# Two-operand masks in layer 1 of a graph attention network: the node index read from a column of PSUM

## The chip, the cores and the metric

The kernel runs on one core of one Trainium2 chip. The metric is the device time of one execution, in microseconds (us); smaller is better. The times given are medians of several executions.

A core has five engines that take their instructions each from a queue of its own, in order: PE (TensorE, the matrix unit, whose weight loads are listed apart as PEld), DVE (VectorE), ACT (ScalarE), POOL (GpSimd) and SP, which here only issues transfers. SBUF and PSUM are the two on-chip memories, of 128 partitions each; matrix products land in PSUM. Sixteen DMA engines move data between DRAM and SBUF. An ordinary DMA is issued by SP or ACT. An *indirect* DMA, which fetches rows of a table by a list of indices, is issued by POOL, and the profile shows it as a POOL instruction (`DMA_INDIRECT`) with a duration.

## What is computed

6250 nodes with 768 features each, 100000 edges (sorted by destination) and a loop on each node. Features are normalised and clipped at zero, then two graph attention layers of 256 channels run over the edges (4 heads, then 1), then two dense layers, and the input is added:

```python
h = jnp.maximum(_layernorm(x, axis=-1), 0.0)
h = relu(gat_conv(h, src, dst, W1, a_src1, a_dst1, b1, heads=4))
h = relu(gat_conv(h, src, dst, W2, a_src2, a_dst2, b2, heads=1))
out = x + relu(h @ Wm1 + bm1) @ Wm2 + bm2

def gat_conv(x, src, dst, W, a_src, a_dst, bias, heads):
    h = (x @ W).reshape(n, heads, -1)
    e = leaky_relu((h * a_src).sum(-1)[src] + (h * a_dst).sum(-1)[dst], 0.2)
    e = exp(e - segment_max(e, dst)[dst])
    alpha = e / (segment_sum(e, dst)[dst] + 1e-16)
    return segment_sum(h[src] * alpha[:, :, None], dst) + bias
```

## The kernel before

**Three stages follow one another.** The first reads the features, normalises them, multiplies by `W1` and stores a table in DRAM: a row of 268 numbers for each node (`store1`, line 499). The second is the attention of layer 1 over the edges; it ends each block of 128 nodes with a product by `W2` and writes a second table (lines 1036 to 1064). The third is the attention of layer 2, with the dense layers and the output.

**Edges come in tiles of 128, four tiles to a group, two groups to a unit.** There are 782 tiles with edges, 196 groups and 98 units; a unit has the edges around one half block of nodes, and four groups make a block step `t`. In both layers `layer_edges` (line 642) runs a loop over the groups. `gather(g)` (line 666) issues one indirect DMA per tile, line 680, which fetches the 128 rows of the table that the tile's edges start from. It is called 8 groups ahead (`AHEAD`), and the tile `G` that takes the rows has 10 buffers. In 23 groups of layer 1 two of the four tiles were fetched during the first stage, from the part of the table that existed then, and laid aside in DRAM (`soon_rows`, `soon_away`); they are loaded back by SP (line 319), and rows that did not exist yet are put in by a one-hot product (`soon_hits` line 333, `soon_missing` line 344, `soon_whole` line 351). So layer 1 has 736 gathers on line 680, layer 2 has 762, and between them stand 20 gathers of line 371 that serve layer 2 in the same manner.

**What a group needs in layer 1.** `make_hot` (line 704) compares the numbers 0 to 127 along a row with the edge's destination: a one-hot matrix, edges by nodes, which adds edge rows up by node on PE. The other direction, a number of the destination node for each edge, takes the transposed one-hot matrix, nodes by edges: that is the *mask*. `make_mask(u)` (line 687) makes it for a unit of 8 tiles: `drow` holds the destinations, taken modulo 128, of 2048 edges in bf16, the same in all partitions (`fetch_rows`, line 640, from SP), and each partition compares them with its own number, `pidx`, a column of SBUF with the values 0 to 127. The result is 128 x 1024 in bf16 and goes to PE in `meet` (line 727), to ACT (line 739) and back to DVE (line 746). Masks are made five to six groups ahead of the group that uses them, one for two groups, in the middle of an iteration (lines 944 to 948).

On DVE a group then has two small operations on the attention factors (lines 761 and 762), the weighting of the gathered rows (line 764, `hw`, which is the last reader of `G`), and on PE the product with the one-hot matrix into `o_ps` (line 784). Line 802 carries sums on from unit to unit.

**Order.** From line 425 on, the instructions of an engine run in the order in which the program issues them; each engine waits on semaphores for what it reads and for buffers to come free.

**Constants in PSUM.** A bank of PSUM, `both_ps` (lines 130 to 139), is divided by `part_ps` into `iota_ps` (0 to 127 along the row), `nid_ps` (node numbers), `mine_ps` and `rden_ps` (work space), and what is left is `own_ps`, which holds, four numbers a block, the weights of the nodes' own loops. `keep_own` (line 1015) fills `own_ps` first and the rest of another bank after it.

Of the kernel before, what the change touches and what calls it, by code (L numbers as in the profile page):

```python
# [14 lines left out]
ALU = mybir.AluOpType  # L15
AX = mybir.AxisListType

P = 128
# [9 lines left out]
NT = -(-N // P)  # L28
# [43 lines left out]
def kernel(  # L72
# [21 lines left out]
    nc = tc.nc  # L94
# [22 lines left out]
    pidx = const.tile([P, 1], F32, name="pidx")  # L117
# [9 lines left out]
    late_nid = min(SOON_FROM, NEXT_FROM)  # L127
    wide = 4 * (HID // 4 + 1)
# [3 lines left out]
    def part_ps(n):  # L132
        at_ps[0] += n
        return both_ps[:, at_ps[0] - n:at_ps[0]]

    iota_ps, nid_ps, mine_ps, rden_ps = (part_ps(n) for n in (P, NT - late_nid, wide, 8))
    own_ps = part_ps(4 * P - at_ps[0])
    nc.vector.tensor_copy(iota_ps, iota)
    nc.vector.tensor_copy(nid_ps, nid[:, late_nid:])
    eps_c = const.tile([P, 1], F32, name="eps_c")  # L140
    nc.vector.memset(eps_c, EPS)
    idle = const.tile([P, 4 * P], BF16, name="idle")
# [483 lines left out]
    drow, mask = {}, {}  # L626
# [15 lines left out]
    def layer_edges(layer, H, node, pre, matched, pre_pool):  # L642
# [4 lines left out]
        with tc.tile_pool(name=f"eg{layer}", bufs=6) as eg, \  # L647
# [36 lines left out]
            def both(u):  # L684
                return tiles(2 * u)[0], TPG + tiles(2 * u + 1)[-1] + 1

            def make_mask(u):

                if layer == 2 or not 0 <= u < NU:
                    return  # L690
                a, b = (t * P for t in both(u))
                mask[u] = maskp.tile([P, 8 * P], BF16, name="mask")
                at = u % 2 * 8 * P
                nc.vector.tensor_scalar(mask[u][:, a:b], drow[u // 2][:, at + a:at + b], pidx, None,
                                        ALU.is_equal)

            def make_hot(g):

# [150 lines left out]
            if layer == 1:  # L849
                fetch_rows(0)  # L850
                soon_away(0)
                for r in range(1, 3):
                    fetch_rows(r)
                soon_sources(pre_pool, 0)
                fetch_rows(3)
                for u in range(4):
                    make_mask(u)
            else:
                next_away()
# [55 lines left out]
            for g in range(NG):  # L915
# [20 lines left out]
                if j == 0:  # L936
                    if layer == 1:
                        fetch_rows(t + 4)
                    node.prefetch(t)
                    if layer == 1:  # L940
                        meet(t + 2 if t > 0 else 1)
                elif j == (2 if t < NT - 1 else 1):
                    node.ahead(t)
                elif j % 2 and (layer == 2 or t > 0):
                    make_mask((g + (11 if layer == 1 else 7)) // 2)
                if layer == 1 and t == 0:
                    for u in ((), (4, 5), (6,), (7,))[j]:
                        make_mask(u)
                    if j == 1:
                        parts_out(1)  # L950
                    if j == 2:
                        meet(2)
# [576 lines left out]
```

## Time and profile before

| | |
|---|---|
| median of 3 executions | 2093.42 us (2092.66 to 2094.27) |
| the profiled execution, its own time | 2094.35 us |
| span of the profile, first to last instruction | 2092.6 us |
| mean granted TensorE clock | 0.918 |
| busy share | PE 77%, PEld 59%, DVE 71%, ACT 20%, POOL 73% |
| first stage | 0 to about 166 us |
| gathers of layer 1 | 166 to 1091 us |
| masks | 98, from 174 to 1036 us |
| gathers of layer 2 | 1116 to 2069 us |

A page of the profile sums busy time by engine, and lists groups of equal instructions with their count, busy time and mean duration in ns; behind the bar stand the idle time of the engine ahead of them and what ended it. Register, branch and semaphore instructions and the issuing of ordinary DMAs do not count as busy. In a timeline each row is one instruction or a run of equal ones: its start and duration in us, the engine, the line, the operation, what it writes `<-` what it reads, and in brackets the idle time before it. "issue" there is time in which the engine waited for nothing that the profile shows.

### The profile page before, as it was taken

How to read it: one execution, taken by the hardware profiler on the slowest of the kernel's cores; microseconds unless marked ns; L12 is line 12 of the kernel's file. 1: busy time of each engine (PE TensorE's matmuls, PEld its weight loads, DVE VectorE, ACT ScalarE, POOL GpSimd, SP SyncE). 2: the span in 40 equal slices, each digit the busy share in tenths (PEclk: the TensorE clock that was granted, in tenths of full speed). 3: DMA queues.
4: the chain of work that ended last, by engine and by line, in shares of the span. 5: the costliest groups of instructions: out<-in, count | busy, mean ns of one | idle time of the engine just before them, and what ended most of it. 6: DMA issues, size and time to landing. Idle time of an engine off the chain costs nothing.

```text
span 2092.6 us, 23253 instructions
## 1 busy us (share of the span) xinstructions
PE 1612.2 (77%) x7207; PEld 1228.4 (59%) x7208; DVE 1491.2 (71%) x2879; ACT 422.9 (20%) x1322; POOL 1521.5 (73%) x1666
## 2 busy tenths in 40 slices
PE   8984879878877887887763787777787787777676
PEld 6873657757666766766652655555555455454444
DVE  7855777777777777777763877777677677676774
ACT  5761111111111111111120111111111111111211
POOL 7067777777777777777777777777777777777774
PEclk9996989989989989999886899999999989999999
DMA  9998555555555555555447355455455555555453
GB/s 346 352 347 289 143 159 155 149 159 156 161 154 150 156 156 164 154 143 163 132 122 219 105 159 160 141 156 159 145 151 160 147 150 159 146 149 152 145 160 104
DMA packets 145643, 354.58 MB, mean 169 GB/s; under 512 B 33943, under 2 KB 57582, under 8 KB 145510
## 3 DMA queue, kind: packets, MB, share of 16 engines
q0 software_dynamic: 75040, 210.90, 36.9%
q1 hardware_dynamic: 69100, 140.62, 19.7%
q10 hardware_dynamic: 1370, 1.48, 0.3%
q8 instruction: 59, 0.97, 0.2%
q14 instruction: 74, 0.61, 0.1%
HBM read 311.29 MB, written 41.59 MB: 169 GB/s over the span
## 4 chain that ended last, share of the span: by engine, by line
POOL 22%; DMA 21%; PE 19%; DVE 19%; issue 17%; ACT 1%; DVEq 0%; SPq 0%; POOLq 0%; ACTq 0%
POOL G L680 22%; DMA G<-table,src_i 18%; PE o_ps L784 8%; PE h_ps L472 4%; DVE u_ps L775 3%; PE missing L344 3%; DVE hw L764 3%; DVE u_ps L777 3%; DVE hot L778 2%; PE y_ps L1184 2%; DVE hot L704 1%; DVE soon_hit L333 1%; DMA xTt<-in_xT 1%; DMA xt<-in_x 1%; PE missing L402 1%
## 5 line engine op out<-in xcount | busy, mean ns | idle before, releaser
L680 POOL DMA_INDIRECT G<-table,src_i x1498 | 1421.6, 949 | 456.3 <-issue 373.2
L784 PE MATMUL o_ps<-G,hot 128*128 128x258 f32 x1564 | 424.1, 418 | 257.1 <-DVE hot L778 256.7
L784 PE MATMUL o_ps<-hw,hot 128*128 128x260 f32 x1564 | 442.3, 436 | 165.7 <-DVE hw L764 138.1
L784 PEld LDWEIGHTS o_ps<-G,hot 128*128 128x128 f32 x1564 | 304.8, 203 | 369.6 <-DVE hot L778 322.4
L784 PEld LDWEIGHTS o_ps<-hw,hot 128*128 128x128 f32 x1564 | 327.1, 215 | 244.8 <-DVE hw L764 152.4
L811 ACT ACTIVATE sum<-acc 32x260 f32<-32x260 f32 (+1 forms) x384 | 160.0, 417 | 1362.0 <-DVE acc L802 1297.6
L775 DVE TENSOR_TENSOR u_ps<-rho_ps,G 128x512 f32<-128x512 f32 (+1 forms) x197 | 136.3, 692 | 234.3 <-DMA G<-table,src_i 163.4
L704 DVE TENSOR_TENSOR hot<-iota_ps,dcol 128x512 f32<-128x512 f32 x392 | 265.7, 679 | 0.0
L764 DVE TENSOR_TENSOR hw<-G,factors 128x1040 f32<-128x1040 f32 (+1 forms) x198 | 242.2, 1223 | 14.3 <-DVE factors L762 0.9
L344 PE MATMUL missing<-kept,soon_hit 128*128 128x268 f32 x1028 | 245.6, 395 | 0.0
L344 PEld LDWEIGHTS missing<-kept,soon_hit 128*128 128x128 f32 x1028 | 196.5, 193 | 36.1
L1184 PE MATMUL y_ps<-wm,mT 128*128 128x384 f32 x392 | 160.1, 533 | 0.8 <-ACT mT L1179 0.8
L761 DVE TENSOR_TENSOR factors<-G,factors 128x16 f32<-128x16 f32 (+1 forms) x198 | 34.5, 174 | 151.4 <-DMA G<-table,src_i 106.9
L472 PE MATMUL h_ps<-w,r 128*128 128x264 f32 (+1 forms) x588 | 137.1, 387 | 6.4 <-ACT r L462 6.3
L777 DVE TENSOR_TENSOR u_ps<-u_ps,G 128x512 f32<-128x512 f32 (+1 forms) x197 | 136.7, 694 | 6.8
L778 DVE TENSOR_TENSOR hot<-hot,u_ps 128x512 f32<-128x512 f32 (+1 forms) x197 | 134.1, 681 | 6.8
L472 PEld LDWEIGHTS h_ps<-w,r 128*128 128x128 f32 x588 | 108.0, 190 | 28.4 <-ACT r L462 9.6
L1184 PEld LDWEIGHTS y_ps<-wm,mT 128*128 128x128 f32 x392 | 70.5, 200 | 50.0 <-issue 25.0
L309 POOL DMA_INDIRECT G<-table,soon_i x46 | 43.7, 949 | 75.7 <-DMA xt<-in_x 53.6
L802 DVE SCALAR_TENSOR_TENSOR acc<-acc,keep,o_ps 128x260 f32<-128x260 f32 (+1 forms) x192 | 91.5, 477 | 5.0 <-PE o_ps L784 5.0
L333 DVE TENSOR_TENSOR soon_hit<-soon_of,iota_ps 128x1408 f32<-128x1408 int32 (+18 forms) x46 | 75.1, 1633 | 0.0
L1188 DVE TENSOR_TENSOR y<-y_ps,xt 128x384 f32<-128x384 f32 (+1 forms) x98 | 54.0, 551 | 26.7 <-PE y_ps L1184 26.3
(428 smaller groups left out, 1317.2 us busy)
## 6 DMA issues: line engine op xcount, KB each, us to landing
xt<-in_x SPq DMA_DIRECT2D x96, 384.0 KB, 5.4
drow<-dmod_d SPq DMA_DIRECT2D x49, 512.0 KB, 5.7
G<-table,src_i POOLq DMA_INDIRECT x1498, 2.8
xTt<-in_xT SPq DMA_DIRECT2D x49, 384.0 KB, 7.4
out<-y SPq DMA_DIRECT2D x48, 384.0 KB, 3.0
table<-kept SPq DMA_DIRECT2D x49, 134.0 KB, 4.3
table<-kept SPq DMA_DIRECT2D x49, 129.5 KB, 3.0
soon_d<-G SPq DMA_DIRECT2D x23, 268.0 KB, 7.7
```

What stands on the lines that cost most here:

```text
L333: nc.vector.tensor_tensor(soon_hit[k][:, :m], soon_of[i][:, t * P:(t + 1) * P].unsqueeze(1).to_broadcast([P, m, P]), nid_ps[:, SOON[i] - l ...
L344: nc.tensor.matmul(soon_p[k], hit[:, T - there], kept[T], start=(T == there), stop=(T == NT - 1))
L472: nc.tensor.matmul(h_ps[:, :n], r[:, k], w1[:, k, :n], start=(k == 0), stop=(k == KI - 1))
L680: nc.gpsimd.indirect_dma_start(out=G[g][:n, t], out_offset=None, in_=table[layer], in_offset=bass.IndirectOffsetOnAxis(ap=src_i[:n, k:k + ...
L704: nc.vector.tensor_tensor(hot[g][:, T[0]:T[0] + n], iota_ps.unsqueeze(1).to_broadcast([P, n, P]), dcol[:, k:k + n].unsqueeze(2).to_broadca ...
L764: nc.vector.tensor_mul(hw[:, of], Gg[:, :, :RW[1]].rearrange("p t (h c) -> p t h c", h=H), w.unsqueeze(3).to_broadcast([P, n, H, C + 1]))
L775: nc.vector.tensor_mul(u_ps[:, of], row.unsqueeze(1).to_broadcast([P, n, P]), e2.to_broadcast([P, n, P]))
L777: nc.vector.tensor_max(u_ps[:, of], u_ps[:, of], e1.to_broadcast([P, n, P]))
L778: nc.vector.tensor_mul(hot[g][:, of], hot[g][:, of], u_ps[:, of])
L784: nc.tensor.matmul(o_ps[u], hot[g][:, k], r, start=(g % 2 == 0 and k == 0), stop=(g % 2 == 1 and k == tiles(g)[-1]))
L811: nc.scalar.activation(done[t][r], acc[r], AF.Copy)
L1184: nc.tensor.matmul(y_ps, mT[:, j], wm2[:, j, s * half:(s + 1) * half], start=False, stop=(j == KH - 1))
```

## The change

A column is set aside in the PSUM bank and filled once, at the start, with the partition's number (`pidx_ps`). `make_mask` no longer compares `drow` with a number per partition (`tensor_scalar`, the number read from `pidx` in SBUF) but with this column, spread over the row with a step of zero, as a second operand (`tensor_tensor`). What comes out is the same. `own_ps` becomes one column narrower, 95 in place of 96, so that it holds the numbers of 23 blocks in place of 24; the others go to the second bank.

```diff
-    iota_ps, nid_ps, mine_ps, rden_ps = (part_ps(n) for n in (P, NT - late_nid, wide, 8))
+    iota_ps, nid_ps, mine_ps, rden_ps, pidx_ps = (part_ps(n) for n in (P, NT - late_nid, wide, 8, 1))
     own_ps = part_ps(4 * P - at_ps[0])
     nc.vector.tensor_copy(iota_ps, iota)
     nc.vector.tensor_copy(nid_ps, nid[:, late_nid:])
+    nc.vector.tensor_copy(pidx_ps, pidx)
...
-                nc.vector.tensor_scalar(mask[u][:, a:b], drow[u // 2][:, at + a:at + b], pidx, None,
-                                        ALU.is_equal)
+                nc.vector.tensor_tensor(mask[u][:, a:b], drow[u // 2][:, at + a:at + b],
+                                        pidx_ps.to_broadcast([P, b - a]), ALU.is_equal)
```

## The prediction

> **What bounds the kernel now.** I read four views: the summary of stages (busy time of each engine in chosen windows), the list of groups, the waits, and last single rows of the timeline. The summary first; its columns are the window, its length, the busy time and count of each engine, the granted clock, the DMA share and GB/s.
>
> ```profile
> 0.00:166.10 166.10, 146.23 (x657) 117.31 (x658) 118.52 (x286) 109.43 (x345) 80.96 (x148) 0.98 0.99 346
> 166.10:1090.70 924.60, 739.25 (x3656) 600.67 (x3656) 680.96 (x1386) 144.17 (x523) 700.44 (x736) 0.90 0.56 158
> 1090.70:1115.70 25.00, 8.48 (x24) 5.52 (x24) 7.10 (x26) 3.76 (x17) 18.92 (x20) 0.62 0.75 206
> 1115.70:2069.00 953.30, 704.41 (x2814) 496.97 (x2815) 676.70 (x1164) 162.03 (x427) 721.16 (x762) 0.93 0.52 152
> 2069.00:2092.60 23.60, 13.85 (x58) 7.89 (x56) 7.91 (x20) 3.56 (x11) 0.00 (x0) 0.95 0.11 36
> ...
> L680 POOL DMA_INDIRECT G<-table,src_i x1498 | 1421.6, 949 | 456.3 <-issue 373.2
> ```
>
> The engines stand in the order PE, PEld, DVE, ACT, POOL. In the first stage the DMA engines are busy at 0.99. After it nothing is: in layer 1 PE has 739 of 925 us, DVE 681, POOL 700. POOL seems to have a quarter of its time free, but the group row of the gathers says that it hasn't: 1498 gathers of 949 ns leave 456 us idle, which is 0.30 us a gather. The table of waits shows that this gap is no wait on another engine:
>
> ```profile
> POOL G L680 <- issue: 373.2, 1225, 0.3
> POOL G L680 <- PE o_ps L784: 20.4, 67, 0.3
> ```
>
> The last number is the longest single idle time: 0.3 us, whichever releaser the view names. So each gather takes its duration and 0.3 us between two, back to back from 166 to 2069 us. POOL's row of gathers is the path of 1903 of the 2093 us, and a microsecond saved in it is one of the total, as long as it stays ahead.
>
> **Where masks touch that row.** Layer 1 and a stretch of layer 2 in which no mask runs, for line 680 alone:
>
> ```profile
> 166.10:1090.70 924.60, 700.44 (x736) 0.90 0.56 158
> 1190.00:2069.00 879.00, 664.67 (x703) 0.95 0.52 152
> ```
>
> A gather in layer 1 takes 700.44 / 736 = 0.9517 us, in layer 2 664.67 / 703 = 0.9455 us. The time from one start to the next is 924.60 / 736 = 1.2563 against 879.00 / 703 = 1.2504 us. By durations layer 1 loses 736 x 0.0062 = 4.6 us, by starts 736 x 0.0059 = 4.3 us. Where it loses them, the rows say:
>
> ```profile
> 166.02 0.36 DVE L620 TENSOR_TENSOR v<-e,rho 128x196 f32<-128x196 f32 x1 [2.02 <-ACT e L618]
> 166.11 1.09 POOL L680 DMA_INDIRECT G<-table,src_i  x1 [0.30 <-issue]
> ...
> 183.76 1.01 POOL L680 DMA_INDIRECT G<-table,src_i  x1 [0.30 <-issue]
> 184.17 0.88 DVE L694 TENSOR_SCALAR mask<-drow,pidx 128x1024 bf16<-128x1024 bf16 x2 [9.23 <-DMA drow<-dmod_d]
> ...
> 378.34 0.47 DVE L694 TENSOR_SCALAR mask<-drow,pidx 128x1024 bf16<-128x1024 bf16 x1
> 378.43 1.21 POOL L680 DMA_INDIRECT G<-table,src_i  x1 [0.30 <-issue]
> 378.74 2.55 DVE L333 TENSOR_TENSOR soon_hit<-soon_of,iota_ps 128x2304 f32<-128x2304 int32 x1
> 379.94 0.95 POOL L680 DMA_INDIRECT G<-table,src_i  x1 [0.30 <-issue]
> ...
> 1035.77 0.98 POOL L680 DMA_INDIRECT G<-table,src_i  x1 [0.30 <-DVE o L1048]
> ```
>
> A gather that starts while a mask is in flight takes 1.21 us in place of 0.95 (at 378.43); one that a mask meets later in its course, 1.01 (at 183.76). I went through all starts of layer 1: up to the last mask 40 gathers are 0.03 us or more late, 39 of them with a mask beside them (the first at 183.76 us, the last at 1035.77), and the other is the very first, 0.14 us late beside line 620, which reads two tensors of SBUF. The 39 come to 4.4 us. The other masks cost POOL nothing; where they ran longer than the 0.47 us of the one at 378.34, they themselves waited:
>
> ```profile
> L694 DVE TENSOR_SCALAR mask<-drow,pidx x98: 407/477/723, 174.0 to 1036.2; 128x1024 bf16<-128x1024 bf16 x97, 128x768 bf16<-128x768 bf16 x1
> ```
>
> These are the shortest, the median and the longest of the 98, in ns (the shortest is the last, of 768 columns). So mask and gather hold something against each other that the next form doesn't: line 333 at 378.74 us compares SBUF with a spread PSUM column in 2.55 us, the very form of the new mask, and the gather that starts under it at 379.94 us takes 0.95 us.
>
> **The change part by part.** *The mask's hold on the gathers goes.* Adding up single gathers gives 4.4 us, the two window sums 4.6 and 4.3, less the 0.14 of line 620: 4.5 and 4.2. I take 4.4 and keep 4.2 to 4.5. The lower bound supposes that the new form holds no gather, as the row of line 333 shows.
>
> *The mask gets longer.*
>
> ```profile
> L694 DVE TENSOR_SCALAR mask<-drow,pidx 128x1024 bf16<-128x1024 bf16 x97 | 49.5, 513 | 15.6 <-DMA drow<-dmod_d 15.6
> ...
> L333 DVE TENSOR_TENSOR soon_hit<-soon_of,iota_ps 128x1024 f32<-128x1024 int32 x2 | 2.4, 1206 | 0.0
> ```
>
> Line 333 at the same 1024 columns takes 1206 ns, with 4-byte elements on both sides. For bf16 against a 4-byte column the trace has no row; the bounds are 513 ns (as now) and 1206, or a little above, and I take 1206, the row nearest in form. That adds 98 x 0.69 = 68 us to DVE in layer 1: 681 becomes 749 of 920 us.
>
> The Trainium skill speaks against the change here: "VectorE: DVE Perf Modes", section "The perf-mode tier table", puts `tensor_scalar` on bf16 in SBUF at four elements a cycle and any `tensor_tensor` with a PSUM operand at one. The rows agree in kind (513 against 1206 ns), and with the whole difference on the path the sum would be the second rival's.
>
> *What hides the 68 us.* Queued behind a mask on DVE are the group's factors and `hw`, and PE's products wait for those; POOL waits for `hw` only through the buffers of `G`. In the view of line 761 in layer 1 (idle time in us, times, by releaser) stands how far DVE keeps up:
>
> ```profile
>   DMA G<-table,src_i: 106.9, 71
> ```
>
> 71 times DVE had nothing to do until a gather landed. Its other large wait, from the view of line 351:
>
> ```profile
>   PE missing L344: 40.3, 20
> ```
>
> How late `hw` comes after its group's last gather, at the worst of the 190 groups that I followed after the start (group 19) and at an ordinary one (group 22):
>
> ```profile
> 260.35 0.95 POOL L680 DMA_INDIRECT G<-table,src_i  x1 [0.31 <-issue]
> ...
> 269.96 1.24 DVE L764 TENSOR_TENSOR hw<-G,factors 128x1040 f32<-128x1040 f32 x1
> ...
> 275.41 0.95 POOL L680 DMA_INDIRECT G<-table,src_i  x1 [0.30 <-DMA G<-table,src_i]
> ...
> 278.81 1.24 DVE L764 TENSOR_TENSOR hw<-G,factors 128x1040 f32<-128x1040 f32 x1
> ```
>
> 8.7 and 2.5 us after the gather's end, and it falls back to 2.4 or so within every eight groups. A gather issued eight groups ahead needs a buffer that was read two groups ago, which leaves it more than 30 us of its 40. A unit, two groups or 10 us, gets 0.69 us longer, out of idle time of (925 - 681 - 40) / 98 = 2.1 us. So `hw` gets later by one or two us at times and POOL does not see it; the cover would be gone at a mask of 0.5 + 2.1 = 2.6 us. At the start of layer 1 seven masks stand close together, 5 us more for DVE, but there some 40 gathers, 50 us, run before one needs a buffer that group 0 has read.
>
> *The new column.* One copy, of one column:
>
> ```profile
> 7.81 3.53 PE L509 MATMUL warm_ps<-idle 128*128 128x512 bf16 x8
> 7.83 0.18 DVE L139 COPY iota_ps<-nid 128x20 f32<-128x20 f32 x1
> ...
> 8.01 0.95 DVE L460 TENSOR_TENSOR cent<-xTt,mean_ps 128x768 f32<-128x768 f32 x1
> ...
> 9.00 0.84 ACT L462 ACTIVATE r<-cent 128x768 f32<-128x768 f32 x1 [0.90 <-DVE cent L460]
> ```
>
> 0.18 us at most, ahead of line 460. What needs that result on PE stands behind warm-up products until 11.34 us, and line 460 and ACT's 0.84 us after it would be done by 10.0: nothing, or 0.18 without that cover. The loops' numbers of block 23 move to the other bank; line 1030 reads them there, and takes 428 ns from either:
>
> ```profile
> L1030 DVE TENSOR_TENSOR iota_ps<-kept,factors 128x260 f32<-128x260 f32 x25 | 10.7, 428 | 0.1
> L1030 DVE TENSOR_TENSOR iota_ps<-kept,iota_ps 128x260 f32<-128x260 f32 x24 | 10.3, 428 | 0.0
> ```
>
> *What is late next.* When layer 1's gathers end sooner, 20 gathers of line 371 follow and then those of layer 2, which need the whole second table.
>
> ```profile
> 1097.52 5.29 SPq L1063 DMA_DIRECT2D table<-kept  x2
> ...
> 1115.76 0.95 POOL L680 DMA_INDIRECT G<-table,src_i  x1 [0.30 <-issue]
> ```
>
> The last store is issued by 1102.8 us, the first gather of layer 2 starts at 1115.76 without a wait. The last mask is at 1036 us, so both ends move together. The 23.6 us after the last gather do not change.
>
> The sum: 2092.6 - 4.4 = 2088.2 us of span, 2089.95 for the profiled execution, whose own time is 2094.35. That execution is 0.9 us above the median, so of the median: 2093.42 - 4.4 = **2089.0 us**, 0.21% less. The three executions before lie 1.6 us apart, and about 0.2%, 4.2 us, is what a measurement of this kernel can tell from no change: the gain sits on that line.
>
> **The rivals.** *The change doesn't do what it says*: any DVE instruction, or the longer one, meets as many gathers, and the masks hold as much as before: 2093.4. Against it stands the gather at 379.94 us; for it, that the new form has run here only on int32 and float32. 7%.
>
> *DVE becomes the bound*: with 68 us on the path, 2093.4 - 4.4 + 68 = 2157. For it: DVE at 74% of layer 1 rises to 81%, with PE waits on top. Against: 0.3 us is POOL's longest wait. 2%.
>
> *The new form takes the shared thing for its whole, longer run*, slower than before. The place is the start of a gather, the price is in these rows:
>
> ```profile
> 1180.40 0.96 DVE L1096 TENSOR_TENSOR drow<-dst_f,wbase 128x784 f32<-128x784 f32 x1
> 1180.75 1.44 POOL L680 DMA_INDIRECT G<-table,src_i  x1 [0.31 <-issue]
> ```
>
> A `TENSOR_TENSOR` of 0.96 us held a gather for 0.49. 98 such holds are 48 us, 2093.4 - 4.4 + 48 = 2137. It decides by whether the second operand comes through the way that gathers use: lines 620 and 1096 read two tensors of SBUF and hold, line 333 reads one of SBUF and one of PSUM and does not, and the new mask is of the second kind. 3%.
>
> The Trainium skill, "SBUF — State Buffer", section "Who interferes with whom", has the same split: an instruction with two SBUF inputs meets GpSimd's reads, one with at most one does not, outside the modes that use two ports. By that rule the hold goes, and the trace agrees (0.95 us at 379.94).
>
> **How the numbers follow.** The forecast has 88%. Around 2089.0 I put half a microsecond of the measured spread and a few tenths for the bounds, so 62% of it lies below 2089.2, the line of 0.2%: faster 0.55, same 0.88 x 0.38 + 0.07 = 0.40, slower 0.05. The range takes 1.7 us below the forecast, and above it nearly three, towards the case without gain: 2087.3 to 2091.8.
>
> **What would show it right or wrong.** Right: no gather of layer 1 above 1.0 us but the first; 920.2 us from the first gather to line 371; the mask's row at 1.2 us; DVE at 749 us in layer 1; POOL's longest wait still 0.3. Wrong: gathers of 1.2 us or more beside a mask (the form holds), or idle time of POOL on `hw` (buffers), or a gap at the first gather of layer 2.

## The result, and the profile after

| | before | changed | ratio, 95% interval |
|---|---|---|---|
| first comparison, 17 executions each | 2092.66 us | 2089.00 us | 0.9982, 0.9976 to 0.9989 |
| second comparison, another chip | 2094.93 us | 2090.57 us | 0.9983, 0.9973 to 0.9993 |

The medians lie 3.7 us apart in the first and 4.4 us in the second comparison; by the ratios the gain is 0.18 and 0.17%. The forecast of 2089.0 us was met. The gain is real, both intervals exclude 1, and it lies at the line of 0.2% as foreseen, though just below it, where the prediction had given the side above the better chance (0.55 against 0.40).

The windows of the changed kernel, cut at its own first gather (165.31 us) and at the first gather of line 372 (1085.64), first for all engines, then a stretch of layer 2 for its line 681 alone, which is line 680 of before:

```profile
165.30:1085.60 920.30, 730.13 (x3656) 595.36 (x3656) 746.83 (x1386) 144.23 (x523) 696.14 (x736) 0.91 0.56 159
...
1185.00:2063.00 878.00, 664.14 (x703) 0.94 0.52 152
```

POOL's 736 gathers of layer 1 take 696.14 us in place of 700.44, which is 0.9459 us each, against 664.14 / 703 = 0.9447 in layer 2: the difference between the layers is gone but for 0.0012 us. From the first gather to the end of the row it is 920.3 us in place of 924.6; in the trace of the second comparison (164.30 to 1085.23) it is 920.9. DVE has 747 us in place of 681 and pays for the change without being on the path. The mask's row in the list of groups:

```profile
L695 DVE TENSOR_TENSOR mask<-drow,iota_ps 128x1024 bf16<-128x1024 bf16 x98 | 118.1, 1207 | 15.1 <-DMA drow<-dmod_d 15.1
```

The views name a bank of PSUM by its tile, so `pidx_ps` stands there as `iota_ps`. 1207 ns is the mean, and the row of line 333 had said 1206. And a mask in flight while gathers start, in the timeline:

```profile
367.08 1.21 DVE L695 TENSOR_TENSOR mask<-drow,iota_ps 128x1024 bf16<-128x1024 bf16 x1
368.07 0.95 POOL L681 DMA_INDIRECT G<-table,src_i  x1 [0.30 <-issue]
```

This gather starts 0.22 us before the mask ends and takes 0.95 us. Of the 98 longer masks 95 are in flight at such a start, and every one of those gathers takes 0.94 to 0.96 us.

The span of the profile fell from 2092.6 to 2087.4, by 5.2 us, which is more than the medians show. Cut at the starts of gathers, the 5.2 are: 0.8 in the first stage, whose end lay anywhere from 164.3 to 167.7 us in the runs below on the chips on which before takes about 2094 us; 4.3 in the gathers of layer 1; 0.5 in those of layer 2, from an effect that was not forecast (below); and 0.5 given back after the last gather.

### The profile page after: what moved, and what is told of

It is laid out like the page before. It is cut to its first block, busy times and chain, and to the rows that moved or that the text cites. A ratio compares the mean times of both kernels' runs of the same rounds, so it can differ in the third digit from the quotient of the medians.

```text
span 2087.4 us, 23253 instructions
## 1 busy us (share of the span) xinstructions
PE 1604.8 (77%) x7206; PEld 1226.5 (59%) x7208; DVE 1557.0 (75%) x2880; ACT 423.1 (20%) x1322; POOL 1517.2 (73%) x1666
## 4 chain that ended last, share of the span: by engine, by line
POOL 21%; PE 21%; DVE 21%; DMA 19%; issue 16%; ACT 1%; DVEq 0%; SPq 0%; POOLq 0%; ACTq 0%
POOL G L681 21%; DMA G<-table,src_i 16%; PE o_ps L785 8%; PE h_ps L473 4%; PE missing L345 4%; DVE hw L765 3%; DVE u_ps L776 3%; DVE u_ps L778 3%; DVE hot L779 2%; DVE soon_hit L334 2%; PE y_ps L1185 2%; DVE hot L705 2%; DVE mask L695 1%; DMA xt<-in_x 1%; PE missing L403 1%
## 5 line engine op out<-in xcount | busy, mean ns | idle before, releaser
L785 PE MATMUL o_ps<-hw,hot 128*128 128x260 f32 x1564 | 435.0, 430 | 169.3 <-DVE hw L765 145.9
L695 DVE TENSOR_TENSOR mask<-drow,iota_ps 128x1024 bf16<-128x1024 bf16 x98 | 118.1, 1207 | 15.1 <-DMA drow<-dmod_d 15.1
L762 DVE TENSOR_TENSOR factors<-G,factors 128x16 f32<-128x16 f32 (+1 forms) x198 | 34.5, 174 | 78.6 <-DMA G<-table,src_i 57.4
```

Source lines behind the costliest of these rows:

```text
L695: nc.vector.tensor_tensor(mask[u][:, a:b], drow[u // 2][:, at + a:at + b], pidx_ps.to_broadcast([P, b - a]), ALU.is_equal)
L785: nc.tensor.matmul(o_ps[u], hot[g][:, k], r, start=(g % 2 == 0 and k == 0), stop=(g % 2 == 1 and k == tiles(g)[-1]))
```

## Experiments

The theory: a gather waits at certain moments while DVE runs an operation of certain forms; the old mask was one of them and the new is not; the longer mask is hidden by DVE's idle time. Rivals: that it matters where the number `pidx` is read rather than the form; that two operands as such are harmless; that the longer mask already eats part of the gain. Four kernels ran first on a chip on which the kernel is slower, and were repeated on others.

### Where the number is read

```diff
-                nc.vector.tensor_tensor(mask[u][:, a:b], drow[u // 2][:, at + a:at + b],
-                                        pidx_ps.to_broadcast([P, b - a]), ALU.is_equal)
+                nc.vector.tensor_scalar(mask[u][:, a:b], drow[u // 2][:, at + a:at + b], pidx_ps, None,
+                                        ALU.is_equal)
```

> The number per partition is read from the PSUM column, but as the scalar of a one-tensor operation, as before the change. Theory (what holds the gathers is the fast run of a one-tensor operation from SBUF to SBUF, wherever its scalar lies): the masks take 0.47 us again, about 40 gathers of layer 1 are late, layer 1's gathers take 924 to 925 us to line 372, the time is that of before, 2092.7. Rival (the SBUF column pidx is what is held): masks of 0.47 us and no late gather, 920.3 us, 2088 to 2089.

> The scalar form with its number read from the PSUM column, once more. Theory (the fast one-tensor run from SBUF to SBUF is what holds gathers, wherever the scalar lies): masks of 0.47 us, 35 to 45 late gathers in layer 1 that come to 3.5 to 5 us, layer 1's gathers 924 to 925.5 us, the time of before within 1.5 us. Rival (reading pidx from SBUF holds them): no late gather beside a mask, 920.3 us, 4 us less than before.

On the slower chip 2604.8 us against 2607.3 of before, ratio 1.0005 (0.9979 to 1.0032), which decides nothing. On the other 2093.52 against 2094.16, ratio 0.9997 (0.9988 to 1.0006): no gain. The windows of line 681 there:

```profile
167.70:1091.40 923.70, 699.46 (x736) 0.91 0.57 158
```

923.7 us, near the 924.6 of before and 3.4 above the changed kernel, a little under the expected 924; 28 gathers beside masks are 0.03 us or more late, by 2.9 us in all, under the expected 35 to 45 and 3.5 to 5 us. One of them:

```profile
352.33 0.48 DVE L695 TENSOR_SCALAR mask<-drow,iota_ps 128x1024 bf16<-128x1024 bf16 x1
352.46 1.17 POOL L681 DMA_INDIRECT G<-table,src_i  x1 [0.30 <-issue]
```

The scalar comes from PSUM and the gather is held as before. So it isn't the reading of `pidx` but the form of the operation, with `drow` and the mask in SBUF.

Rows of the trace before narrow down what the form is. Line 1150 is a one-tensor operation, too, as long as the old mask, with input and scalar in SBUF, but its result goes to PSUM:

```profile
1365.13 0.48 DVE L1150 TENSOR_SCALAR iota_ps<-kept,own 128x258 f32<-128x258 f32 x1
...
1365.26 0.95 POOL L680 DMA_INDIRECT G<-table,src_i  x1 [0.30 <-issue]
```

Seven times it was in flight for 0.18 us or more past the start of a gather, and no gather was late. `hw` (line 764), which reads `G` in SBUF and a factor in PSUM, ran on for 0.2 us or more past the start of 169 gathers, and none was late. One-tensor operations from SBUF to SBUF do not all hold either: a copy of 1.37 us on 32 partitions (line 611) ran on for 1.25 us past a gather's start at 161.11 us, and that gather took 0.94 us. So the operation's name and length are not what holds; whether it is the quick rate of the mask alone, no run here separates.

### Both operands in SBUF

```diff
-                                        pidx_ps.to_broadcast([P, b - a]), ALU.is_equal)
+                                        pidx.to_broadcast([P, b - a]), ALU.is_equal)
```

> The new form with the column spread from SBUF in place of PSUM: a two-operand operation with both operands in SBUF. Theory (an operation that reads two tensors of SBUF holds a gather that starts under it until it ends, as lines 620 and 1096 did): masks of about 1.2 us, gathers of layer 1 held by up to 1 us each beside a mask, 35 to 60 us more than the changed kernel, 2125 to 2150. Rival (only the fast one-tensor run holds, two operands never do): no late gather, 2088 to 2089.

> The two-operand form with both operands in SBUF, once more. Theory (it holds a gather that starts under it until it ends): the 98 masks held 90 gathers by 41 us in all in the trace of the slower chip, and here gathers are the path, so layer 1's gathers take about 961 us and the time is 37 us above before, 2122 to 2140. Rival (its holds are absorbed as the changed kernel's longer masks are): within 2 us of the changed kernel.

On the slower chip 2635.5 us, ratio 1.0105 (1.0050 to 1.0159). On the other 2130.08, ratio 1.0172 (1.0156 to 1.0187): 36 us slower than before, within the expected 2122 to 2140, and by that some 40 slower than the changed kernel, which did not run on that chip. The one difference from the changed kernel is that the spread column lies in SBUF; the mask takes 1217 ns, hardly more. The 736 gathers of layer 1 take 735.37 us:

```profile
165.38:1124.99 959.61, 735.37 (x736) 0.89 0.55 153
```

Two of them in the timeline:

```profile
212.48 1.22 DVE L695 TENSOR_TENSOR mask<-drow,pidx 128x1024 bf16<-128x1024 bf16 x1
212.60 1.91 POOL L681 DMA_INDIRECT G<-table,src_i  x1 [0.30 <-issue]
...
240.92 1.22 DVE L695 TENSOR_TENSOR mask<-drow,pidx 128x1024 bf16<-128x1024 bf16 x1
241.62 1.34 POOL L681 DMA_INDIRECT G<-table,src_i  x1 [0.30 <-issue]
```

The first mask ends at 213.70, 1.10 us after the gather's start, and the gather is 0.96 us late; the second ends at 242.14, 0.52 us after, and the gather is 0.39 late. Through the 80 late gathers of the run goes one line: each is late by the mask's end less the gather's start less 0.11 to 0.13 us. It is late as if it waited from 0.12 us after its start until the operation ends. This is the third rival of the prediction, made real by one operand: the place (the start) and the mechanism were right, and 80 late gathers gave 39 us where the rival had put 98 at 48.

The Trainium skill, "SBUF — State Buffer", section "Who interferes with whom", separates one SBUF input from two in the same way, and the runs agree. It also says that an operation in a two-port mode and a GpSimd instruction block each other fully, whichever starts second. Only part of that shows here: a gather waits at some moments of its course, and 59 of the 98 old masks cost it nothing. That the old mask ran in such a mode no run shows by itself.

### How much longer a mask may be

The changed kernel with every mask made two times, and three times:

```diff
+                for _ in range(2):
-                nc.vector.tensor_tensor(mask[u][:, a:b], drow[u // 2][:, at + a:at + b],
-                                        pidx_ps.to_broadcast([P, b - a]), ALU.is_equal)
+                    nc.vector.tensor_tensor(mask[u][:, a:b], drow[u // 2][:, at + a:at + b],
+                                            pidx_ps.to_broadcast([P, b - a]), ALU.is_equal)
```

> The changed kernel with every mask made twice: 118 us more for DVE in layer 1, 749 becomes 867 of 920 us. Theory (the longer mask is covered by DVE's idle time up to 2.6 us for a unit, here 2.4): layer 1's gathers stay at 920 to 922 us, the time at 2089 to 2091. Rival (the longer mask already costs part of the gain, some 0.7 of the 4.4 us): at least twice that loss again, 922 us or more in layer 1 and idle time of POOL on hw, 2091 or more.

> The changed kernel, beside the kernel before on one chip. Theory (POOL's row of gathers is the path where gathers follow one another without a wait): where the kernel before takes about 2093 us, 4.4 us less, layer 1's gathers in 920.3 us. Where it takes about 2607, as beside the first four experiments, gathers wait for hw there (193 us in the run with the scalar in PSUM), so DVE's work is part of the path and the longer masks cost: the doubled masks added 28 us there with 98 x 1.9 = 186 us more of DVE than before, so 68 us more should add about 10, 0.3 to 0.5%. Rival (the change gains by itself, whatever bounds): 4 us less on either.

> The changed kernel with every mask made twice, once more, beside the changed kernel on the same chip. Theory (cover up to 2.6 us for a unit): where the kernel before takes about 2093 us, the same time as the changed kernel within 2 us, layer 1's gathers at 920 to 922 us. Where it takes about 2607, some 18 us more than the changed kernel. Rival (the longer mask already costs part of the gain): at least 2 us more than the changed kernel on the faster chip, with idle time of POOL on hw.

> The changed kernel with every mask made three times, 3.6 us for a unit. With the doubled masks, 2.4 us, the weighting hw came up to 39 us after its gather and only the last gather of layer 1 waited, 10.6 us, so the cover ends near 2.3 us. Theory: 1.3 us for each of 98 units too much, 130 us, of which the buffers hide some 40 until the end of layer 1, where they are paid: 2200 to 2225, POOL waiting on hw in the middle of layer 1. Rival (DVE's order, not its load, made the last gather wait): some 10 to 20 us above before, no waits of POOL in the middle.

On the slower chip the doubled masks took 2635.6 us, ratio 1.0095 (1.0077 to 1.0113). The next pair ran on a chip on which before took 2094.93: the changed kernel 2090.57, and the doubled masks 2097.41, ratio 1.0010 (1.0000 to 1.0019). That is 6.8 us more than the changed kernel; the expectation of at most 2 failed, and the rival's figure, at least 2, came true. But its reason, a cost that single masks already have and POOL idle on `hw`, isn't what the trace shows. No gather of layer 1 waits longer than 0.3 us but the very last:

```profile
1096.68 0.28 DVE L680 MEMSET G<- 128x268 f32 x1
...
1097.23 0.88 POOL L681 DMA_INDIRECT G<-table,src_i  x1 [10.86 <-DVE factors L763]
```

The last tile has fewer than 128 edges, so `gather` first lets DVE zero its part of `G` (line 680), and this stands in DVE's queue behind everything that DVE has not yet done. With doubled masks DVE was busy for 857 us of the layer's 931, `hw` came 19 to 39 us after its group's last gather, where the changed kernel, after the start, has 2.4 to 11. The buffers of `G`, filled eight groups or some 40 us ahead, kept this from the other gathers; the last one paid 10.6 us. The profiled execution took 2103.9 us, the slowest of ten; the median one, 2097.4, must have paid less, which no trace shows.

Three masks a unit took 2216 us (one execution), within the expected 2200 to 2225. Layer 1's gathers took 1046.3 us, and the table of waits has POOL waiting on DVE now:

```profile
POOL G L681 <- DVE hw L766: 101.6, 37, 5.0
```

(1046.3 - 920.3) / 98 = 1.29 us too much for each unit, so by an estimate a mask of 3 x 1.215 - 1.29 = 2.4 us would be the limit for the steady part, near the forecast 2.6. For the end of the layer it lies lower, below the doubled 2.4 us, which already cost 6.8. At 1.2 us the changed kernel is clear of both.

### Twice the old masks

```diff
+                for _ in range(2):
-                nc.vector.tensor_scalar(mask[u][:, a:b], drow[u // 2][:, at + a:at + b], pidx, None,
-                                        ALU.is_equal)
+                    nc.vector.tensor_scalar(mask[u][:, a:b], drow[u // 2][:, at + a:at + b], pidx, None,
+                                            ALU.is_equal)
```

> The kernel before with every mask made twice, in the old form: 98 more operations of 0.47 us. Theory (each such operation holds a gather now and then, 0.045 us in the mean): about 4 us more, layer 1's gathers 928 to 930 us, 2096 to 2098. Rival (the loss in layer 1 isn't the masks' but that of something that runs beside them): no change, 924 to 925 us, 2092 to 2094.

> The old form, every mask twice, once more. Theory (each such operation may hold a gather): late gathers beside masks come to 6 to 10 us in place of 4.4, layer 1's gathers 926 to 930 us, 2 to 5 us above before. Rival (the loss is not the masks'): 924.6 us, no change.

On the slower chip 2617.4 us, ratio 1.0028 (1.0005 to 1.0052), where DVE's added work may cost by itself (next section). On the other 2094.57 against 2094.16, ratio 1.0002 (0.9993 to 1.0011), and layer 1's gathers took 925.8 us:

```profile
165.80:1091.60 925.80, 701.56 (x736) 0.90 0.57 158
```

A miss: 98 more operations of the holding form added 1.2 us, not 2 to 5. In the trace 39 gathers of layer 1 are late beside masks, as many as before, by 5.1 us in all in place of 4.4. So a hold has no price per operation. What counts is where in the gather's 1.25 us an operation falls. Of the second masks 25 began less than 0.03 us before a gather, 22 of them behind a first mask that had waited itself, and none of the 25 made that gather late, though each was in flight for more than 0.4 us of it. The time of this run can't be told from no change, as its rival had it; that the form holds gathers rests on the other runs, not on this one.

### The slower chip

Beside the first four runs before took 2607.28 us (19 executions), on another chip than the rest. The gathers are as quick there, but they do not follow one another without a wait. With the scalar in PSUM, POOL waits 192.8 us for `hw` (line 765), in 43 waits of up to 12.8 us. The granted TensorE clock in layer 1 is 0.79 there in place of 0.91 (the same kernel on the other chip), and a product of line 785 takes 470 ns in place of 429. Engines there also stand still for many microseconds at a time with no cause that the profile names. There DVE is part of the path, and doubled masks cost 28 us at once. What the change itself does on that chip was not measured; by those 28 us for 98 x 1.9 us of DVE its 68 us more would make it slower by about 10 us, which is an estimate only. The cause of that chip's slowness stays open.

## Why the prediction was right

**The bound.** POOL's row of gathers was the path: in the changed kernel, too, no gather of layer 1 waits more than 0.3 us, and with both operands in SBUF, 39 us of late gathers in place of the 4.4 of before made the kernel 36 us slower than before. With masks three times as long the bound moves to DVE, as the argument needs.

**The hold.** 4.2 to 4.5 us were forecast, 4.3 came off the row of layer 1, 3.7 in the second trace, 3.7 and 4.4 off the medians. Its cause stands on four kernels that differ in this one operation: scalar from SBUF or from PSUM, held; two operands in SBUF, held for longer; one in SBUF and one in PSUM, not held.

**The longer mask.** 1206 ns forecast, 1207 measured; 68 us more for DVE forecast, 66 measured in layer 1. `hw` was to come one or two microseconds later at times: at the worst of the same 190 groups 11.1 us after the gather in place of 8.7. DVE's wait for gathers in layer 1 (line 762, line 761 of before) fell accordingly: 57.4 us in 47 waits, where it had been 106.9 in 71.

**Smaller steps.** The first gather of layer 2 still does not wait: 25.0 us lie between the first of the 20 gathers and it, before and after. The column's copy at the start and the loops' numbers in the other bank leave no mark.

**What was off.** That the median met 2089.0 us to the last digit is partly luck: the kernel before took 0.8 us less in the comparison (2092.66) than the 2093.42 that the sum started from, and the gain was 0.7 us smaller than forecast. Two terms were missing. Lines 1096 and 1099 (now 1097 and 1100) had held two gathers of layer 2 by 0.49 and 0.23 us; after the change they meet the gathers at another moment and hold one:

```profile
1176.66 0.56 DVE L1100 TENSOR_SCALAR drow<-dst_f 128x784 f32<-128x784 f32 x1
1176.92 1.12 POOL L681 DMA_INDIRECT G<-table,src_i  x1 [0.30 <-issue]
```

That gave 0.5 us in this profile, and it is chance: in the second trace of the changed kernel the two lines again hold two gathers, by 0.18 and 0.22 us, and the rest after the last gather gave 0.5 back in this one. The second is the cover: the forecast of 2.6 us averaged DVE's idle time over the layer and left out the end, where a zeroing in DVE's queue stands ahead of the last gather. It made no difference at 1.2 us and 6.8 us at twice that.

## What to carry over

Before an engine's row of equal instructions is taken as fixed, compare it between a stage with and one without a suspected neighbour: 0.006 us a gather was visible here in two sums, and the late gathers then led to the operation. A slower form of an operation can be the better one where its engine has room and the quick form holds up the engine on the path; how much room there is, is best measured by making the work two and three times as long, and looked for at the end of a stage as well as in its middle. A hold of this kind has no price per operation; it depends on when the two meet, so that adding or moving other work may change it.

## Hardware behaviour that was not expected

A gather of 128 rows held by a two-operand operation with both inputs in SBUF (1.2 us) is late as if it waited for nothing until 0.12 us after its start, and then until that operation has ended; over 80 late gathers the 0.12 varies from 0.11 to 0.13. Such an operation that was in flight later in a gather's course, and over by the next one's first tenth of a microsecond, cost nothing. The quick one-tensor operation (0.47 us) held gathers at that moment and at a second one: started 0.38 to 0.47 us into the gather it made it late by 0.04 to 0.12 us; started from about 0.47 to 0.7 it waited itself, up to 0.25 us, and the gather was on time.

In the trace before, 17 of the 39 late gathers are of the first kind, 2.6 us in all, and 22 of the second, 1.8 us. An operation that begins just before a gather does not hold it: of the quick ones none that began less than 0.09 us before it did (1 in the trace before, 6 with the scalar in PSUM, 26 with the old masks doubled), and of the two-operand ones the only one that began less than 0.03 us before it did not.
